# Layer 0 of a four-layer kernel: the first convolution one step later, and the small projection's copy at the head of ScalarE's step 0

## The chip, the core and the metric

The kernel runs on one core of a Trainium2 chip. The core has five engines that each work through their own list of instructions in order and wait for one another by semaphores: TensorE (PE, matrix products), VectorE (DVE), ScalarE (ACT, activation functions and copies), GpSimd (POOL) and SyncE (SP, which issues the DMAs here). The metric is the time of one execution on the device in microseconds (us), as a median over several runs.

## The reference

Four layers follow each other on an image of 2 x 128 channels x 64 x 64. The change lies in the first, layer 0: a Mamba block that is run over the 4096 pixels in four orders (by rows and by columns, each forward and reversed) for each of the two images.

```python
xz = x @ W_in.T;  xh, z = jnp.split(xz, 2, axis=-1)      # 256 + 256 channels
xc = depthwise_conv(xh, conv_w, taps=4) + conv_b
xh = silu(xc)
x_dbl = xh @ W_xp.T                                      # the small projection
dt = softplus(x_dbl[..., :8] @ W_dt.T + b_dt)
Bm, Cm = x_dbl[..., 8:24], x_dbl[..., 24:40]
dA = exp(dt[..., None] * A)                              # 256 channels x 16 states
dBu = dt[..., None] * Bm[:, :, None, :] * xh[..., None]
h_t = dA_t * h_{t-1} + dBu_t                             # a scan over 4096 pixels
y = einsum(h, Cm) + xh * Dp
y = y * silu(z)                                          # the gate
out = y @ W_out.T                                        # then fused over the four orders
```

Before it stands a layernorm over the channels. Layers 1 to 3 (two attention layers and another Mamba layer) are not touched.

## The kernel before

**Tiling.** A chunk is 512 consecutive pixels of one order of one image; there are 2 images x 4 orders x 8 chunks = 64 chunks, numbered 0 to 63. Of each eight, the orders alternate: chunks 0 to 7, 16 to 23, 32 to 39 and 48 to 55 run forward, the others reversed. The 256 channels x 16 states of a chunk are cut into 16 units of 128 partitions x 1024 elements, one unit for each step of the loop (`for s in range(16)`). The order of instructions on each engine is the order of the program text: the loop stands in a manual schedule, and nothing reorders it.

**One step `s` of chunk `c`** issues, in this order: on GpSimd the input term of unit s+2 (`s_dbu`, L330); on VectorE the scan of unit s (`s_scan`, L374), then what the table `V` holds for the step, then the product of unit s-1 with C (`s_hc`, L386; for units 0, 5, 9, 11 and 14 it is on GpSimd instead, L384); on ScalarE the decays of unit s+1 (`s_da`: two exponentials, L343), a correction of one column that carries the state from the chunk before (`s_fix`, L355 and L358), a copy of the last state (`s_hst`, L379), and then what the table `A` holds for the step; on TensorE the sums over states (`s_y`, L397, four units in two halves) and what the table `M` holds for the step, and in odd steps the spreading of C for the two next units (`s_pc`, L363).

**Where units wait for each other.** The decays have two buffers (PSUM), so the decays of unit s+1 wait for the end of scan s-1. The input terms have three, so that of unit s+3 waits for scan s. The sums of units 0 to 7 go to one PSUM bank `y`, which VectorE reads in step 10 (the gate of the first half, `yg_(0)`, L404), and those of 8 to 15 to the same bank, which VectorE reads in step 1 of the next chunk (`yg_(1)`, L404). The pairs of units are summed in steps 3, 5, 8, 9, 12, 14, 15 and, for the last pair, in step 1 of the next chunk: a pair waits for both products.

**Preparing later chunks.** The tables hold the work for the next chunk (`new`) and the one after it (`nxt`). All of it passes through one PSUM bank, `misc`: a matmul writes it, and another engine has to read it before the next matmul may write. For `nxt`: the convolution with its projection of channels 0 to 127 (`px(0)`, four matmuls that the trace shows as eight, L228) in step 8, its copy by ScalarE (`x_(0)`, L237) in step 9; `px(1)` in step 10 and `x_(1)` in step 12; the silu of both in step 13 (`xsilu`, L251); the small projection (`pd`, L267) at the end of step 15. For `new`: in step 0, behind decays, correction and state copy, ScalarE's copy of the small projection (`xd_`, L272), with two DMA stores to DRAM by SP (`rows`); then TensorE's `pt(0)` (L287) that reads this copy, in step 0, `pt(1)` in step 1, the absolute values (`abs_`, L294), `exp` and `ln` in steps 1 to 3, `pt` again in 4 and 5, `dt_` on VectorE (L306) in 5 and 6. TensorE's `pt(0)` stands ahead of the sums of the last pair in step 1. Forward chunks also gate `z` in step 8 (`zsilu`, L255, with two loads of an activation table).

**Layernorm chunks.** In chunks 0 to 3 and 15 to 22 part of the layernorm for later pixels runs as well (`ln`: `center` in step 12, `sub` on VectorE in 13, `square` in 14, `var` and `keep` in 14 and 15), and in the chunk after each of them (1 to 4 and 16 to 23) the rest (`lp`: `ln` and `exp` in step 3, `rows` in 6, `scale` in 7, `mul` on VectorE in 8, `affine` on ScalarE in 10).

## Time and profile before

| | us |
|---|---|
| median of 5 runs (6806.72 to 6814.91) | 6812.0 |
| the profiled execution | 6806.72 |
| its span on the core | 6804.9 |
| layer 0 within the span, first scan to last (57.2 to 3470.6) | 3413.4 |
| VectorE idle from 57 to 3468 | 142.5 |
| GpSimd idle from 57 to 3468 | 142.2 |

The page of the profile has a table of busy times, the span in slices, the chain of waits, and groups of instructions by line. A group's row reads: line, engine, operation, out<-in by the program's names, shapes, count | busy us, mean ns of one | idle time of the engine just before it, and what ended that idle time. A timeline row reads: start us, duration us, engine, line, operation, out<-in, shapes, count, and in brackets the engine's idle time before it with what ended it. The granted clock (PEclk) is the share of TensorE's full clock that the core let through.

### The profile page before, as it was taken

To read this page: it belongs to the slowest core of one execution; us is meant where nothing else is said; L and a number is where in the kernel's file an instruction comes from. 1 tells how busy PE (TensorE), PEld (TensorE's weight loads), DVE (VectorE), ACT (ScalarE), POOL (GpSimd) and SP (SyncE) were. 2 spreads that over 40 slices of the span, in tenths; PEclk is the share of its full clock that TensorE was granted. 3 is DMA by queue.
4 is the path that set the end of the run, shared out by engine and by line. 5 is a ranking of instruction groups with operands and counts; after the bars stand their busy time and mean duration, and the time that the engine had idled before them with its cause. 6 is when DMAs were issued, how large, how long until landed. Compare 5 with 4: busy or idle time off the path is not lost. (4 is left out here: it accounts for less than half of the span.)

```text
span 6804.9 us, 67303 instructions
## 1 busy us (share of the span) xinstructions
PE 5996.8 (88%) x20652; PEld 2820.5 (41%) x20652; DVE 5523.6 (81%) x4499; ACT 4457.0 (65%) x7666; POOL 5359.8 (79%) x2487
## 2 busy tenths in 40 slices
PE   8888888888888888888879999999999997888888
PEld 2222222222222222222238887787788884222222
DVE  7999999999999999999966665565566675787777
ACT  7887788877788777887745664555456554434342
POOL 6899998899999999999956664555566666777776
PEclk7777777777777777777779999999999998988888
DMA  6555655566566656565630000000000001222222
GB/s 170 138 149 145 158 147 137 139 156 147 145 157 152 154 144 156 151 154 145 150 91 2 4 4 1 1 1 1 1 1 13 1 1 61 74 72 71 90 75 67
DMA packets 352652, 616.51 MB, mean 91 GB/s; under 512 B 72473, under 2 KB 74786, under 8 KB 351650
## 3 DMA queue, kind: packets, MB, share of 16 engines
q1 hardware_dynamic: 351552, 610.44, 35.0%
q8 instruction: 162, 2.65, 0.2%
q14 instruction: 200, 1.64, 0.1%
q10 hardware_dynamic: 738, 1.78, 0.1%
HBM read 496.45 MB, written 115.47 MB: 90 GB/s over the span
## 5 line engine op out<-in xcount | busy, mean ns | idle before, releaser
L330 POOL TENSOR_TENSOR dbu<-dus,bs 128x1024 f32<-128x1024 f32 x1024 | 2401.5, 2370 | 154.6 <-DVE h L374 138.4
L374 DVE TENSOR_TENSOR_SCAN h<-da,hst,dbu 128x1024 f32<-128x1024 f32 x896 | 2092.7, 2343 | 76.1 <-ACT dbu L358 72.7
L343 ACT ACTIVATE da<-dts,aneg 128x512 f32<-128x512 f32 (+1 forms) x2048 | 1411.4, 689 | 443.7 <-DVE h L374 404.7
L890 POOL TENSOR_TENSOR sum<-sum,sc 128x1024 f32<-128x1024 f32 x384 | 906.1, 2360 | 497.6 <-ACT sc L885 494.0
L852 ACT COPY sc<-s 128x512 f32<-128x512 f32 x1024 | 597.0, 584 | 868.8 <-PE s L847 754.3
L859 DVE TENSOR_TENSOR mx<-mx,s 128x512 f32<-128x512 f32 x896 | 610.0, 681 | 569.4 <-ACT sc L852 568.4
L847 PE MATMUL s<-q,k 128*128 128x256 f32 x4096 | 1058.0, 382 | 11.7 <-ACT q L833 8.4
L902 PE MATMUL av<-sc,v 128*128 128x256 f32 x4096 | 1049.7, 379 | 2.3 <-ACT sc L885 2.3
L397 PE MATMUL y<-hc,cst 128*32 128x512 f32 x4096 | 813.3, 763 | 177.5 <-DVE hc L386 104.1
L386 DVE TENSOR_TENSOR hc<-h,pc 128x1024 f32<-128x1024 f32 x704 | 843.1, 1198 | 0.1
L847 PEld LDWEIGHTS s<-q,k 128*128 128x128 f32 x4096 | 781.2, 192 | 146.2 <-issue 36.6
L902 PEld LDWEIGHTS av<-sc,v 128*128 128x128 f32 x4096 | 769.1, 190 | 103.2 <-ACT sc L885 3.7
L384 POOL TENSOR_TENSOR hc<-h,cs 128x1024 f32<-128x1024 f32 x320 | 756.9, 2365 | 1.3 <-issue 1.3
L363 PE MATMUL pc<-xd,sel 16*128 16x512 f32 x1024 | 713.0, 788 | 4.4 <-DVE hc L386 3.9
L1217 POOL TENSOR_TENSOR A<-A,D 128x1024 f32<-128x1024 f32 x224 | 525.7, 2364 | 225.5 <-DVE D L1222 201.6
L882 DVE TENSOR_TENSOR sc<-sc,pm 128x1024 f32<-128x1024 f32 x512 | 620.9, 1213 | 0.9 <-PE pm L878 0.9
L885 ACT ACTIVATE sc<-sc 128x1024 f32<-128x1024 f32 x512 | 542.1, 1059 | 8.6 <-DVE sc L882 8.1
L287 PE MATMUL misc<-xd,w_dt 9*128 9x512 f32 x504 | 389.8, 862 | 161.0 <-ACT x L426 85.1
L1210 ACT ACTIVATE A<-dtr,aneg 128x1024 f32<-128x1024 f32 (+1 forms) x256 | 245.8, 1031 | 380.6 <-PE y L1242 363.1
L397 PEld LDWEIGHTS y<-hc,cst 128*32 128x32 f32 x4096 | 105.1, 117 | 743.5 <-issue 332.0
L1228 DVE TENSOR_TENSOR A<-A,q 128x1024 f32<-128x1024 f32 (+1 forms) x256 | 276.8, 1081 | 148.7 <-PE q L1194 148.6
L1194 PE MATMUL q<-xs,lb 32*128 32x512 f32 x896 | 331.6, 713 | 72.0 <-DVE D L1204 65.7
(263 smaller groups left out, 8056.9 us busy)
## 6 DMA issues: line engine op xcount, KB each, us to landing
dts<-ddt SPq DMA_DIRECT2D x512, 256.0 KB, 5.4
dus<-ddu SPq DMA_DIRECT2D x512, 256.0 KB, 5.0
bs<-rows SPq DMA_DIRECT2D x1024, 64.0 KB, 4.9
cs<-rows SPq DMA_DIRECT2D x1024, 64.0 KB, 3.2
ddt<-dt SPq DMA_DIRECT2D x128, 256.0 KB, 2.0
ddu<-dtu SPq DMA_DIRECT2D x128, 256.0 KB, 4.1
dtr<-ddt SPq DMA_DIRECT2D x448, 64.0 KB, 1.9
rx<-ddx SPq DMA_DIRECT2D x448, 64.0 KB, 1.9
```

The source lines that it names most:

```text
L330: nc.gpsimd.tensor_mul(t, self.dus[q], _bc(self.bs[g], 1, [P, 2, T]))
L343: act(t[:, i, sl], self.dts[q][:, i, sl], AF.Exp, scale=an[:, g, 2 * q + i : 2 * q + i + 1])
L363: mm(t, lhsT=sel[32:48, 4 * g : 4 * g + 4, :].rearrange("p n d -> p (n d)"), rhs=self.xd[32:48, :], start=True, stop=True)
L374: nc.vector.tensor_tensor_scan(ho, ai, bi, init, ALU.mult, ALU.add)
L384: nc.gpsimd.tensor_mul(t, self.h[u], _bc(self.cs[gq(u)[0]], 1, [P, 2, T]))
L386: nc.vector.tensor_mul(t, self.h[u], _bc(self.pc[u // 2], 1, [P, 2, T]))
L397: mm(self.y[q // 2][r : r + 32, :], lhsT=sum4, rhs=self.hc[u][:, i, :], start=False, stop=(u % 8 >= 6), skip_group_check=True)
L847: mm(p[:, o, :], lhsT=j.k[m // 8][:, m % 8 * P : m % 8 * P + P], rhs=self.q, start=True, stop=True)
L859: nc.vector.tensor_max(self.mx, self.s[0][:, 0:2, :] if u == 1 else self.mx, self.p[u])
L882: nc.vector.tensor_sub(s, s, _bc(self.pm[:, :], 1, [P, 4, NQ]))
L890: nc.gpsimd.tensor_add(self.sum, self.s[0] if w == 1 else self.sum, self.s[w])
L902: mm(self.av, lhsT=self.job.v[m // 8][:, m % 8, :], rhs=self.s[u // 2][:, m % 4, :], start=(m == 0), stop=(m == 31))
```

## The change

Three edits in the loop over chunks. `px(0)` of `nxt` moves from table entry 8 to 9 and its copy `x_(0)` from 9 to 10, behind `affine` where there is one. `xd_` leaves the table and is called at the head of ScalarE's part of step 0, ahead of the decays of unit 1. The block with `y0` and `s_y` is written ahead of ScalarE's part instead of behind it.

```diff
                 if new is not None:
-                    A[0] = (new.xd_,)
                     M[0], A[1] = lambda: new.pt(0), (lambda: new.abs_(0),)
...
                 if nxt is not None:
-                    M[8], A[9] = lambda: nxt.px(0), (lambda: nxt.x_(0),)
+                    M[9], A[10] = lambda: nxt.px(0), (lambda: nxt.x_(0),)
                     M[10], A[12] = lambda: nxt.px(1), (lambda: nxt.x_(1),)
...
-                    A[10] = (lp.affine,)
+                    A[10] = (lp.affine, *A.get(10, ()))
...
                     if s in G:
                         G[s]()
 
+                    if s in (3, 11):
+                        c.y0(s // 11)
+                    for cy, e in ((c, s), (old, s + 16)):
+                        for u in pairs.get(e, ()) if cy is not None else ():
+                            cy.s_y(u)
+                            cy.s_y(u + 1)
+
+                    if s == 0 and new is not None:
+                        new.xd_()
                     if c1 is not None:
                         c1.s_da(u1)
                         c1.s_fix(u1)
...
                     for f in A.get(s, ()):
                         f()
 
-                    if s in (3, 11):
-                        c.y0(s // 11)
-                    for cy, e in ((c, s), (old, s + 16)):
-                        for u in pairs.get(e, ()) if cy is not None else ():
-                            cy.s_y(u)
-                            cy.s_y(u + 1)
                     if s in M:
                         M[s]()
```

In the built program TensorE's list changes in one place of each chunk (the eight matmuls of `px(0)` stand behind the sums of units 6 and 7 instead of ahead of them), ScalarE's in two (`xd_` ahead of the decays in step 0, `x_(0)` one step later). The lists of VectorE, GpSimd and SP keep their order, and no instruction is added or removed.

## The prediction

> **What bounds the kernel now.** The edits touch layer 0 alone, so I first took its stretch of the span in the table of windows (columns: PE, PEld, VectorE, ScalarE, GpSimd busy, granted clock, DMA share, GB/s), then the waits of VectorE and GpSimd in it.

> ```profile
> 57.00:3468.00 3411.00, 2887.47 (x7750) 797.15 (x7750) 3268.47 (x2003) 2746.68 (x5231) 3268.77 (x1470) 0.77 0.60 148
> ...
> POOL dbu L330 <- DVE h L374: 138.4, 135, 2.5
> ...
> DVE h L374 <- ACT dbu L358: 72.7, 128, 1.4
> DVE dt L404 <- PE y L397: 38.5, 34, 2.3
> DVE dt L404 <- issue: 18.2, 9, 2.5
> ```

> VectorE and GpSimd are each busy for 3268 of 3411 us (96%) and idle for 142; GpSimd's idle time is nearly all a wait for the scan, so VectorE leads. Its idle time is what an edit can win: 72.7 us before scans, for ScalarE's correction (L358), and 57.1 before the gate (L404), for the sums. Nothing above that can be gained; but any new wait of VectorE adds to the time at once.

> Next I read where these waits lie, chunk by chunk, in the timeline. The gate waits 34.2 us in step 1 and 22.9 in step 10; in step 10 nearly all of it (22.7) is in the eleven chunks 1 to 4 and 16 to 22. The scan waits 22.4 us in step 5 (24 chunks, mostly reversed) and 29.1 in step 15.

> Step 0 of chunk 21, which stands for the twelve chunks 1 to 4 and 16 to 23:

> ```profile
> 1198.79 2.89 PE L267 MATMUL misc<-xs,m 128*73 128x512 f32 x4
> ...
> 1197.07 0.26 ACT L175 ACTIVATE r<-misc,eps 128x4 f32<-128x4 f32 x1
> 1197.22 1.40 ACT L343 ACTIVATE da<-dts,aneg 128x512 f32<-128x512 f32 x2
> 1198.56 0.28 ACT L355 ACTIVATE df<-aneg,dts 128x4 f32<-128x4 f32 x1
> 1198.94 0.39 ACT L358 ACTIVATE dbu<-hst,dbu,df 128x1 f32<-128x1 f32 x1
> ...
> 1201.72 0.68 ACT L272 ACTIVATE xd<-misc,vec 73x512 f32<-73x512 f32 x1 [2.31 <-PE misc L267]
> ...
> 1200.49 2.34 DVE L374 TENSOR_TENSOR_SCAN h<-da,hst,dbu 128x1024 f32<-128x1024 f32 x1
> 1204.64 0.69 DVE L404 TENSOR_TENSOR dt<-sz,y 128x512 f32<-128x512 f32 x1 [1.80 <-PE y L397]
> ```

> ScalarE uses the time in which the small projection (L267) is not ready for the decays of unit 1, and still waits 2.31 us for it afterwards. Scan 1 runs at 1200.49, well ahead of the copy.

> **The copy first in step 0.** One instruction of 0.68 us moves ahead of two decays, the correction and the state copy; it adds no work. Its two stores go out on SP at the same place of SP's list; what reads them is issued from step 8 on, 27 us later, so they cost nothing. What counts is what is now queued behind a wait for the small projection: the decays of unit 1, and scan 1 behind them.

> Chunk 21: ScalarE is free at 1197.33 and now waits for the projection until 1201.72. The copy ends at 1202.40, where it ends today, so `pt(0)`, the sums and the gate's input gain nothing. Decays to correction take 2.11 us (1197.22 to 1199.33): ready at 1204.5. Scan 1 starts 4.0 us late, ends at 1206.8, the gate follows without its 1.80 of wait, and scan 2 comes at about 1207.4 instead of 1205.24: 2.2 lost. I did this sum at each of the 62 chunk boundaries with ScalarE's free time, the projection's end, scan 1 and the gate's wait: 2.2 in eleven of these twelve and 1.5 in chunk 16, together 26.

> Reversed chunks are of two kinds. Chunk 59 (first three lines) and chunk 28 (last two; of the projection's four matmuls the stretch that I asked for holds the last alone):

> ```profile
> 3209.05 2.98 PE L267 MATMUL misc<-xs,m 128*73 128x512 f32 x4
> 3212.27 0.68 ACT L272 ACTIVATE xd<-misc,vec 73x512 f32<-73x512 f32 x1
> 3213.40 2.34 DVE L374 TENSOR_TENSOR_SCAN h<-da,hst,dbu 128x1024 f32<-128x1024 f32 x1
> ...
> 1576.95 0.59 PE L267 MATMUL misc<-xs,m 128*73 128x512 f32 x1
> 1579.69 0.68 ACT L272 ACTIVATE xd<-misc,vec 73x512 f32<-73x512 f32 x1
> ```

> In chunk 59 the projection ends at 3212.03 (2.0 us after scan 0 begins), at a granted clock of 0.57; in 28 it ends at 1577.54 (0.1 after), at 1.00. Late: the copy ends at 3212.75, 0.2 earlier than today, the correction at 3214.9, scan 1 is 1.5 late, and ScalarE is through with step 0 2.0 later. Step 5 of such chunks waits for ScalarE (1.06 here), so ScalarE's lag passes to VectorE. 19 of the 27 reversed boundaries are late, lags of 1.5 to 2.2, 38 in all, less 0.6 of gate waits: +37. Early: nothing is lost, and in six chunks a gate wait of 1.26 goes, of which 0.56 comes back in step 5 (the wait there of chunk 28, which has no gate wait): 6 x 0.7 = -4. Together +33.

> Forward chunks without layernorm: 17 boundaries, 8 late by 0.5 to 0.9 net (+6.0), 9 early with gate waits of 0.5 to 1.06 that go (-7.4): -1.4. The six chunks that begin a row of eight: +2.5. The copy's move sums to 26 + 33 - 1.4 + 2.5 = +60. Bounds: if every projection is late, 26 + 27 x 2.1 + 17 x 0.9 + 4 = +102; if every one is early, see the first rival.

> **The convolution behind the sums.** Eight matmuls of L228 move behind the sums of units 6 and 7, and one copy of 0.69 us goes from step 9 to 10. Chunk 20:

> ```profile
> 1171.06 1.94 PE L397 MATMUL y<-hc,cst 128*32 128x512 f32 x8
> 1172.92 5.63 PE L228 MATMUL misc<-xnt,wk 128*128 128x512 f32 x8
> 1178.49 1.06 PE L397 MATMUL y<-hc,cst 128*32 128x512 f32 x8
> 1180.53 3.70 PE L228 MATMUL misc<-xnt,wk 128*128 128x512 f32 x8
> ...
> 1178.59 0.69 ACT L237 ACTIVATE xs<-misc,vec 128x512 f32<-128x512 f32 x1 [4.02 <-PE misc L228]
> ...
> 1179.68 0.69 DVE L404 TENSOR_TENSOR dt<-sz,y 128x512 f32<-128x512 f32 x1 [2.46 <-issue]
> ```

> In the eleven chunks, gate and decays of unit 11 both wait behind the first convolution: 2.46 us, and 0.56 more at scan 11. With the sums ahead, the gate's input is there at 1174.9. But TensorE does the same work without a gap from 1171 to the mean for the layernorm in step 12, which ends at 1188.2, and VectorE's subtraction of step 13 needs it; that subtraction starts at 1188.8 today. So of 3 us only 0.6 to 0.8 can be kept: 11 x 0.7 = -8. The bounds are -3.0 and +1.0 a chunk (the convolution at half clock for two rows more).

> In the 20 forward chunks the step-10 and step-11 waits are 0.2 to 0.4 us; I take -0.2 each, -4. Queued behind the copy in step 10 are now the decays of unit 12. In reversed chunks there is no wait to win, and the convolution starts later: chunk 59 runs it at 3237.99, and the product of unit 7 ends at 3242.06, so it starts at 3243.1 after a gap in TensorE. At full clock (3.70) after a slow start it ends at about 3247.7, its copy at 3248.4, and the deadlines hold: the spread of C for unit 10 is due at 3250.4, the second convolution's copy at 3252.3. Cover: 0. At half clock throughout it takes 3.70 x 1.94/1.06 = 6.8, ends at 3249.9, and with 1.1 for the spread and 3.70 for the second convolution the second copy ends 2.4 later than today; scan 15 waits 0.63 for ScalarE already, so at most 2.4 is lost. Range 0 to 2.4 x 31 = 74; I take 0, since the clock was 0.55 up to 1178.5 and 1.00 right after it in chunk 20, that is, it rose within such a convolution.

> [...]

> Moving the block of `s_y` in the text changes no engine's order by itself: 0.

> **Sum.** 60 - 8 - 4 = +48 on the profiled execution's 6806.7 (span 6804.9 and 1.8 around it): 6855. The median stands 5.3 above it: 6860.

> **Rivals.** First (not slower, it can be faster): the later convolution fills TensorE's list through steps 11 to 13, the clock stays up and every projection is early. Then reversed chunks give -5, forward ones -8, the twelve lose 1.45 less each (half of 2.89), +9, the convolution -12: -16, 6796. It decides once the projection runs at clock 1.00 at nearly all boundaries. For it: chunk 28; against: the two kinds alternate today, and a longer chunk shifts them. Chance 0.14. Second (no change): the clock stays up in plain chunks, but the twelve keep their 26: 26 - 5 - 8 - 12 = +1, 6813. Chance 0.14. Third (slower still): the convolution runs at half clock in the reversed chunks: +48 + 74 = 6934 at most. For it: the gap; against: the rise in chunk 20. Chance 0.17. The change not doing what it says is part of my forecast: at the boundaries where the copy waits for the projection today, putting it first makes it no earlier.

> **Chances.** My forecast, late copies at half the boundaries, has 0.55 and its own range 6830 to 6890. With the rivals the range is 6796 to 6918: it leaves out the lower half of the first and the upper half of the third, some 0.15. Differences under 0.2% (13.6 us) can't be told from none: faster 0.12 (the first rival but for its end near zero), same 0.16 (that end and the second), slower 0.72 (forecast and third).

> **What would show it.** ScalarE's copy (L272) waiting for L267 in most chunks, 1.5 to 4.4 us each, against 26.7 us in all today; the first decays of step 0 behind it; scan 1 waiting for L358 by 3 to 4 us in the twelve chunks; the gate's waits gone; the subtraction (L161) waiting for its mean. I am wrong if L272 waits for less than 60 us in all, or if L386 and scan 15 in reversed chunks wait much longer than today.

## The result and the profile after

| | before | after |
|---|---|---|
| median, us | 6814.76 (47 runs) | 6815.38 (27 runs) |
| ratio, 95% interval | | 1.0003 [0.9998, 1.0009] |
| profiled execution, us | 6806.72 | 6798.98 |
| layer 0, first scan of chunk 0 to first scan of chunk 63 | 3363.5 | 3375.1 |

No change that can be measured, where I had forecast 48 us more. Layer 0 itself did get longer, by 11.6 us in the profiled executions. Both figures repeat within 0.8 us in a second profile of each kernel (3363.7 and 3374.3), so this is no accident of one execution.

The table of windows for layer 0 after the change (columns as before: PE, PEld, VectorE, ScalarE, GpSimd busy, granted clock, DMA share, GB/s), and the list of waits:

```profile
57.00:3468.00 3411.00, 2885.17 (x7727) 790.11 (x7727) 3256.15 (x1998) 2730.09 (x5222) 3258.79 (x1465) 0.78 0.60 148
```

```profile
ACT xs L237 <- PE misc L228: 118.0, 53, 3.7
DVE h L374 <- ACT dbu L358: 69.5, 117, 1.3
ACT xs L237 <- PE y L390: 67.7, 56, 2.0
ACT xd L272 <- PE misc L267: 56.3, 19, 5.0
DVE h L374 <- ACT hst L379: 42.8, 12, 4.5
...
DVE xc L161 <- PE misc L157: 16.6, 12, 2.0
...
DVE hc L386 <- PE y L397: 8.6, 18, 0.8
```

(A row of waits: who waited and for whom, us in total, number of waits, longest us.) Three things are to be seen. VectorE's busy time in the same stretch fell by 12.3 us: so much more of it is now waiting. The waits of the gate (L404) are gone from the list, 57 us of them. In their place stand twelve waits of a scan for ScalarE's state copy (42.8 us), the subtraction (L161, 16.6) and the products (L386, 8.6). And the small projection's copy (L272) waits only 19 times, not "in most chunks".

Sorted by kind of chunk, each from its first scan to the next chunk's (plain means without layernorm; "first" are the six chunks after chunk 0 that begin a row of eight and have none; a projection is late if it ends over 0.5 us after scan 0 begins):

| | twelve layernorm chunks | 17 forward plain | 6 first | 27 reversed | late at 50 plain boundaries |
|---|---|---|---|---|---|
| before, us | 681.7 | 900.1 | 301.5 | 1429.2 | 31 |
| after, us | 694.9 | 897.0 | 306.8 | 1425.0 | 1 |
| difference | +13.2 | -3.1 | +5.3 | -4.2 | |
| predicted | +26 - 8 | -1.4 - 4 | +2.5 | +33 | |

The error of 37 us lies in the reversed chunks. The step into chunk 60 in the timeline of the kernel after; scan 15 and scan 0 stand as one row of two, so scan 0 begins at about 3273.6:

```profile
3271.20 1.94 PE L267 MATMUL misc<-xs,m 128*73 128x512 f32 x4
...
3271.35 4.59 DVE L374 TENSOR_TENSOR_SCAN h<-da,hst,dbu 128x1024 f32<-128x1024 f32 x2 [1.20 <-ACT dbu L358]
...
3273.40 0.68 ACT L272 ACTIVATE xd<-misc,vec 73x512 f32<-73x512 f32 x1
...
3276.97 2.35 DVE L374 TENSOR_TENSOR_SCAN h<-da,hst,dbu 128x1024 f32<-128x1024 f32 x1
...
3279.23 0.66 DVE L404 TENSOR_TENSOR dt<-sz,y 128x512 f32<-128x512 f32 x1
```

The projection takes 1.94 us, at a granted clock of 1.00, and ends before scan 0 begins. ScalarE copies it without a wait, scan 1 and the gate have none either. What is paid is the 1.20 in front of scan 15, where before it was 0.63 (ahead of chunk 59). The step into chunk 60 had its projection early before the change, too; the one into chunk 59, which the prediction shows as late, is now early:

```profile
3219.14 1.94 PE L267 MATMUL misc<-xs,m 128*73 128x512 f32 x4
```

It ends 0.6 us before scan 0 begins at 3221.63. Before, it took 2.98 us and ended 2.0 us after scan 0 began.

In a layernorm chunk (21, which begins at 1210.03) it went as I had worked it out:

```profile
1210.30 3.62 PE L267 MATMUL misc<-xs,m 128*73 128x512 f32 x4 [0.20 <-ACT r L175]
...
1213.96 0.68 ACT L272 ACTIVATE xd<-misc,vec 73x512 f32<-73x512 f32 x1 [3.71 <-PE misc L267]
1214.54 1.40 ACT L343 ACTIVATE da<-dts,aneg 128x512 f32<-128x512 f32 x2
...
1216.74 2.35 DVE L374 TENSOR_TENSOR_SCAN h<-da,hst,dbu 128x1024 f32<-128x1024 f32 x1 [3.25 <-ACT hst L379]
...
1219.01 0.66 DVE L404 TENSOR_TENSOR dt<-sz,y 128x512 f32<-128x512 f32 x1
```

The copy waits 3.71 us for the projection, the decays of unit 1 stand behind it, and scan 1 waits 3.25; the gate no longer waits.

### The profile page after: what moved, and what is told of

It is laid out like the page before. It is cut to its first block, busy times and chain, and to the rows that moved or that the text cites. A ratio compares the mean times of both kernels' runs of the same rounds, so it can differ in the third digit from the quotient of the medians.

```text
span 6797.2 us, 67302 instructions
## 1 busy us (share of the span) xinstructions
PE 5991.3 (88%) x20652; PEld 2812.8 (41%) x20652; DVE 5516.3 (81%) x4499; ACT 4445.8 (65%) x7666; POOL 5360.7 (79%) x2487
## 5 line engine op out<-in xcount | busy, mean ns | idle before, releaser
L330 POOL TENSOR_TENSOR dbu<-dus,bs 128x1024 f32<-128x1024 f32 x1024 | 2401.1, 2370 | 165.6 <-DVE h L374 148.4
L374 DVE TENSOR_TENSOR_SCAN h<-da,hst,dbu 128x1024 f32<-128x1024 f32 x896 | 2093.0, 2343 | 114.9 <-ACT dbu L358 69.5
L343 ACT ACTIVATE da<-dts,aneg 128x512 f32<-128x512 f32 (+1 forms) x2048 | 1410.3, 689 | 369.6 <-DVE h L374 331.2
L397 PE MATMUL y<-hc,cst 128*32 128x512 f32 x4096 | 908.1, 761 | 209.5 <-DVE hc L386 202.5
L386 DVE TENSOR_TENSOR hc<-h,pc 128x1024 f32<-128x1024 f32 x704 | 844.0, 1199 | 11.8 <-PE y L397 8.6
L363 PE MATMUL pc<-xd,sel 16*128 16x512 f32 x1024 | 696.9, 771 | 1.6 <-DVE hc L386 1.3
L397 PEld LDWEIGHTS y<-hc,cst 128*32 128x32 f32 x4096 | 126.7, 120 | 881.9 <-DVE hc L386 462.1
L287 PE MATMUL misc<-xd,w_dt 9*128 9x512 f32 x504 | 349.7, 779 | 131.7 <-ACT x L426 59.6
```

What stands on the lines that cost most here:

```text
L330: nc.gpsimd.tensor_mul(t, self.dus[q], _bc(self.bs[g], 1, [P, 2, T]))
L343: act(t[:, i, sl], self.dts[q][:, i, sl], AF.Exp, scale=an[:, g, 2 * q + i : 2 * q + i + 1])
L363: mm(t, lhsT=sel[32:48, 4 * g : 4 * g + 4, :].rearrange("p n d -> p (n d)"), rhs=self.xd[32:48, :], start=True, stop=True)
L374: nc.vector.tensor_tensor_scan(ho, ai, bi, init, ALU.mult, ALU.add)
L386: nc.vector.tensor_mul(t, self.h[u], _bc(self.pc[u // 2], 1, [P, 2, T]))
L397: mm(self.y[q // 2][r : r + 32, :], lhsT=sum4, rhs=self.hc[u][:, i, :], start=False, stop=(u % 8 >= 6), skip_group_check=True)
```

## The experiments

The theory at this point: the copy in front costs time where the projection is late, the later convolution makes the projections of the plain chunks early, and in the layernorm chunks it gains more than I gave it. The rival: the copy's move itself, with the delays that it makes, changed the clock. The first four kernels take the change apart.

**The convolution's move alone.**

```diff
-                    M[8], A[9] = lambda: nxt.px(0), (lambda: nxt.x_(0),)
+                    M[9], A[10] = lambda: nxt.px(0), (lambda: nxt.x_(0),)
...
-                    A[10] = (lp.affine,)
+                    A[10] = (lp.affine, *A.get(10, ()))
```

> The kernel before with the convolution's move alone (px(0) in step 9, x_(0) in step 10); the small projection's copy stays behind the decays. Theory (the convolution's move keeps TensorE at full clock until the small projection, and the copy's move costs about 2 us in each of the twelve layernorm chunks): at nearly all of the 50 plain boundaries the small projection ends within 0.5 us of scan 0, as with the whole change (1 late of 50), against 31 late of 50 before; layer 0 is 10 to 25 us shorter than with the whole change and 0 to 15 us shorter than before, so 6795 to 6812 us beside 6814. Rival (the early projection comes from the copy's move, the convolution's move does nothing outside the layernorm chunks): 20 or more of the 50 boundaries stay late and the time is that of before within 5 us.

Measured: 6826.95 against 6807.87, 1.0027 [1.0015, 1.0038]. One projection of 50 is late, so this move makes them early, and the rival falls. But the time did not follow: the twelve get shorter by 25.8 us, the reversed chunks longer by 29.4 and the first ones by 9.6. A reversed chunk in its timeline, steps 9 to 15 of chunk 60 (which begins at 3275.87):

```profile
3309.19 5.40 PE L228 MATMUL misc<-xnt,wk 128*128 128x512 f32 x8
...
3315.57 3.70 PE L228 MATMUL misc<-xnt,wk 128*128 128x512 f32 x8
...
3320.17 0.69 ACT L237 ACTIVATE xs<-misc,vec 128x512 f32<-128x512 f32 x1 [1.45 <-PE y L390]
...
3322.21 1.22 DVE L386 TENSOR_TENSOR hc<-h,pc 128x1024 f32<-128x1024 f32 x1 [0.59 <-PE y L397]
...
3327.84 1.94 PE L267 MATMUL misc<-xs,m 128*73 128x512 f32 x4
...
3328.07 4.59 DVE L374 TENSOR_TENSOR_SCAN h<-da,hst,dbu 128x1024 f32<-128x1024 f32 x2 [1.27 <-ACT dbu L358]
```

The first convolution takes 5.40 us, the second starts late, its copy holds ScalarE for 1.45 (the row names L390, the matmuls that follow the second convolution on TensorE), a product waits 0.59 and scan 15 waits 1.27. And in step 0 of the same chunk the small projection's copy still stands behind the decays:

```profile
3273.38 1.94 PE L267 MATMUL misc<-xs,m 128*73 128x512 f32 x4
...
3275.99 1.41 ACT L343 ACTIVATE da<-dts,aneg 128x511 f32<-128x511 f32 x2 [0.24 <-DVE h L374]
...
3278.10 0.68 ACT L272 ACTIVATE xd<-misc,vec 73x512 f32<-73x512 f32 x1
...
3278.82 2.07 PE L287 MATMUL misc<-xd,w_dt 9*128 9x512 f32 x2 [2.46 <-ACT xd L272]
...
3280.83 1.94 PE L397 MATMUL y<-hc,cst 128*32 128x512 f32 x8
...
3282.83 0.69 DVE L404 TENSOR_TENSOR dt<-sz,y 128x512 f32<-128x512 f32 x1 [1.26 <-PE y L397]
```

The projection is ready at 3275.3 and is copied at 3278.1; `pt(0)` and the sums follow it, and the gate waits 1.26. Early projections alone help nobody as long as the copy comes last in step 0.

**The copy's move alone.**

```diff
-                    A[0] = (new.xd_,)
...
+                    if s == 0 and new is not None:
+                        new.xd_()
                     if c1 is not None:
                         c1.s_da(u1)
```

> The kernel before with the copy's move alone. Theory: the small projection stays late at about half of the 50 plain boundaries, ScalarE waits for it with the decays queued behind, and the +60 us of the prediction's arithmetic appear: 6850 to 6880 us, with about 26 of them in the twelve layernorm chunks and 33 in the reversed ones. Rival (the lost time at ScalarE is made up elsewhere and the sum of the prediction was wrong by itself): 6815 to 6830 us, layernorm chunks longer by less than 15 us in all.

Measured: 6839.56, 1.0050 [1.0038, 1.0063]. Now all 27 reversed projections are late. Its list of waits:

```profile
ACT xd L272 <- PE misc L267: 132.3, 54, 5.2
DVE h L374 <- ACT hst L379: 87.0, 45, 4.5
```

This is the picture that I had predicted for the change as a whole: a wait of the copy at nearly every boundary and 87 us of scans behind it. Yet it costs 31.5 us in layer 0 and not 60 to 102. The idle time of VectorE by kind of chunk and step shows why (us; sums over the chunks of the kind, worked out from the gaps in the traces):

| | before | convolution alone | copy alone | after |
|---|---|---|---|---|
| reversed, step 1: scan | 0 | 0 | 46.2 | 0 |
| reversed, step 1: gate | 8.1 | 31.5 | 0 | 0 |
| reversed, step 5: scan | 19.9 | 0 | 2.2 | 6.5 |
| reversed, step 13: product | 0 | 10.2 | 0 | 6.0 |
| reversed, step 15: scan | 15.7 | 30.4 | 15.7 | 30.3 |
| reversed, all steps | 52.0 | 76.5 | 64.5 | 47.3 |
| layernorm, step 1: scan | 0 | 0 | 39.6 | 46.2 |
| layernorm, step 1: gate | 17.3 | 14.0 | 0 | 0 |
| layernorm, steps 10 and 11: gate and scan | 28.9 | 0 | 23.2 | 0 |
| layernorm, step 13: subtraction | 0 | 10.6 | 0 | 15.2 |
| layernorm, all steps | 55.7 | 31.2 | 72.7 | 69.4 |

In reversed chunks a late scan 1 takes the place of waits in steps 1, 3 and 5: 46 us new, 33 gone. And the two moves repair each other: the convolution makes the projection early, so the copy in front has no wait (46.2 to 0); the copy in front takes the gate's wait away that the convolution alone brings (31.5 to 0). The singles sum to 15.4 + 31.5 = 46.9 us in layer 0; together they cost 11.6.

**The whole change, but with the copy in its old place in the twelve layernorm chunks.** Against the kernel after:

```diff
+                    if lp is not None:
+                        A[0] = (new.xd_,)
...
-                    if s == 0 and new is not None:
+                    if s == 0 and new is not None and lp is None:
                         new.xd_()
```

> The whole change, but in the twelve chunks that finish a layernorm (1 to 4, 16 to 23) the copy keeps its old place behind the decays. Theory: the twelve chunks lose the wait of scan 1 (47 us over 12 chunks, of which 26 us were a net loss) and the rest stays as with the change: 15 to 30 us under the change, 6785 to 6800 us. Rival (the layernorm chunks are bound by TensorE through step 13 anyway, the 47 us only replace other waits): within 8 us of the change.

Measured: 6769.07, 0.9949 [0.9936, 0.9962]: faster than the kernel before. Layer 0 is 3337.1 us (3375.1 with the whole change), the twelve 655.6. Against the kernel after this is 39.3 us less in the twelve alone, and so that is the price of the copy in front there once the convolution stands late: 46.2 of scans and 4.4 more before the subtraction, less 11.8 of gate waits (this kernel's own, in the twelve).

**The copy alone, with `px(1)` issued twice in plain chunks**, to keep TensorE busy late in the chunk without the convolution's move.

```diff
+                    if ln is None and lp is None:
+                        M[10] = lambda: (nxt.px(1), nxt.px(1, nxt.px_))
```

> The copy's move alone, and in chunks without layernorm work the second convolution (four matmuls, 3.7 us at full clock) is issued twice over the same bank, which adds work for TensorE and nothing for any other engine. Theory (what makes the projection early is a TensorE that is busy through steps 10 to 13 and so keeps its clock): late projections at plain boundaries fall under 15 of 50 and the time falls under that of the copy's move alone by 15 us or more, in spite of the added matmuls. Rival (order and not the clock makes the projection early): late boundaries stay at 25 or more and the time is that of the copy's move alone or up to 30 us longer.

Measured: 6855.81, 1.0072 [1.0060, 1.0084]. The late projections fell from 37 to 17 of 50, between the two expectations, so more work does bring them forward; but the time is 16 us above that of the copy alone, as the rival allowed, since the extra work holds back the sums that the products wait for:

```profile
DVE hc L386 <- PE y L397: 32.2, 19, 2.2
```

The added work is too large to separate the two effects; the experiment with the z projections below adds less.

**The later convolution in the twelve layernorm chunks alone**, nothing else changed.

```diff
-                    M[8], A[9] = lambda: nxt.px(0), (lambda: nxt.x_(0),)
+                    w = 9 if lp is not None else 8
+                    M[w], A[w + 1] = lambda: nxt.px(0), (lambda: nxt.x_(0),)
...
-                    A[10] = (lp.affine,)
+                    A[10] = (lp.affine, *A.get(10, ()))
```

> The kernel before with the convolution's move in the twelve chunks that finish a layernorm alone (1 to 4, 16 to 23), the copy in its old place everywhere. Theory (the convolution's move wins 26 us in the layernorm chunks and loses 29 us in the reversed ones, where it had no wait to remove): layernorm chunks 682 to 656 us, the reversed ones as before (1429 within 5), late projections in the reversed chunks as before (about 19 of 27), layer 0 shorter by 20 to 30 us; 6780 to 6795 us beside 6808. Rival (the gain in the layernorm chunks hangs on what the move does to the clock in the whole layer): layernorm chunks gain less than 13 us.

Measured: 6775.56, 0.9953 [0.9941, 0.9966]. The twelve take 656.4 (-25.3), the reversed 1429.6 (+0.4), and the projections are late as before (28 of 50). So the gain in the twelve is their own, and no matter of the clock elsewhere. The timeline and the windows of its chunk 20, which begins at 1125.49:

```profile
1156.53 3.34 PE L397 MATMUL y<-hc,cst 128*32 128x512 f32 x16
1159.80 3.70 PE L228 MATMUL misc<-xnt,wk 128*128 128x512 f32 x8
```

```profile
1146.00:1159.40 13.40, 10.83 (x26) 2.40 (x26) 13.40 (x10) 11.57 (x23) 13.33 (x7) 0.50 0.50 132
1159.40:1179.00 19.60, 16.82 (x56) 5.93 (x52) 18.57 (x12) 16.85 (x34) 18.90 (x9) 1.00 0.85 218
```

The clock rises at 1159.4, 33.9 us into the chunk (38.0 with the whole change, where the chunk begins with the copy's wait). Before, the convolution took 5.63 us, at a granted clock of 0.65 over its length, as the clock rose only 37.7 us into the chunk. Here it finds the clock up and takes 3.70. That is the 1.9 us a chunk which my sum "TensorE does the same work" left out.

**The split version, with `x_(1)` copied in step 13 instead of 12 where the next chunk is reversed.** It is aimed at the wait that remains, of scan 15.

```diff
                     A[13] = (nxt.xsilu,)
+                    if new.rev and ln is None:
+                        A[13] = (*A.pop(12), nxt.xsilu)
```

> The split version (whole change, copy in its old place in the layernorm chunks), and in reversed chunks without layernorm the second convolution's copy moves from step 12 to step 13, behind the decays of unit 14. Theory (with the convolution later, ScalarE waits in step 12 for the second convolution with the decays of unit 14 queued behind, which makes the wait of scan 15 in reversed chunks 1.27 us instead of 0.63): the wait of scan 15 falls from 49 us to about 30 us in all and the reversed chunks by 10 to 17 us; 5 to 20 us under the split version. Rival (the wait of scan 15 is set by the table loads and silu of step 13 and not by the copy ahead of them): the wait stays at 45 us or more, the time within 5 us of the split version.

Measured: 6772.73, 0.9950 [0.9935, 0.9964]. VectorE's wait in step 15 falls from 49.1 to 35.6 us over layer 0, but the reversed chunks lose only 4.8. Part of what they gain in step 15 (30.1 to 20.4) comes back before scan 5 (5.6 to 10.5). Layer 0 is 10.5 us shorter than in the split version, and the time is the same within the intervals: the wait moved as the theory said, the time as the rival did. The wait of that copy more than halves, from 67.6 us in the split version to

```profile
ACT xs L237 <- PE y L390: 28.6, 27, 2.0
```

**The copy alone, with two z projections (results not read) in step 13 where the next chunk is reversed.** Against the kernel with the copy alone:

```diff
+                    if new.rev and ln is None:
+                        M[13] = lambda: (nxt.pz(0), nxt.pz(1, nxt.pz_))
```

> The copy's move alone, and in the chunks ahead of a reversed chunk two matmuls of the z projection are issued in step 13 into the free bank and never read: work for TensorE where it was idle, on nobody's path. Theory (the projection is early when TensorE was busy through step 13 and so ran at full clock): late projections in reversed chunks fall from 27 of 27 to under 8, the granted clock in the last 5 us of these chunks is over 0.9, and the reversed chunks take 1400 to 1430 us against 1441 with the copy's move alone. Rival (the order of the convolution makes it early, the clock follows): 20 or more stay late and the reversed chunks take 1441 us or longer.

Measured: 6816.33, 1.0014 [1.0005, 1.0023], 10.5 us above the kernel before as timed beside it, where the copy alone was 31.7 above, although TensorE does more. Of the 27 reversed projections 16 are late, where with the copy alone all 27 were; the result lies between the two expectations for the count, and the reversed chunks (1426.0) are where the theory had them. The waits behind the copy:

```profile
ACT xd L272 <- PE misc L267: 99.9, 54, 5.2
DVE h L374 <- ACT hst L379: 55.0, 31, 4.5
```

(132.3 and 87.0 with the copy alone.) The granted clock over the last 5 us ahead of the reversed chunks is 0.89 on the mean, 0.50 with the copy alone (0.64 before, 1.00 after). So two z projections more in step 13 raised the clock ahead of the projection from 0.50 to 0.89, but not at every boundary: 16 of 27 stay late.

**The kernel before and the kernel after once more**, without an edit, to see what repeats.

> The kernel before, profiled once more. Theory: layer 0 repeats within 3 us (3363.5 us from the first scan of chunk 0 to that of chunk 63), and the rest of the span varies by 10 us or more, which is why 12 us in layer 0 did not show in the ratio. Rival: layer 0 itself varies by 10 us or more between executions, so the 12 us are no effect of the change.

> The whole change once more, profiled and timed. Theory: layer 0 repeats (3375.1 us from the first scan of chunk 0 to that of chunk 63, within 3 us) and is 12 us longer than before, while the time after layer 0 differs between executions by up to 27 us (3317 to 3342 us in the traces so far), so that the ratio lies between 0.999 and 1.003. Rival: the time after layer 0 is shorter with the change by about as much as layer 0 is longer, in every execution: it stays near 3317 us in this trace too.

Measured: the kernel before 6797.09 in its one run, the kernel after 6815.7 against 6811.52, 1.0004 [0.9995, 1.0013]. Layer 0 repeats within 0.2 and 0.8 us, and the sums of every kind of chunk within 2.2. What is left of the span from the end of the last scan does not repeat: 3334.3 and 3324.0 us before, 3316.7 and 3332.9 after.

**The later copy of `x_(1)` in all chunks without layernorm.** Only the condition of the experiment above changes.

```diff
-                    if new.rev and ln is None:
+                    if ln is None:
```

> As the version that copies the second convolution in step 13 in the reversed chunks, but in all chunks without layernorm. Theory (the wait of scan 15 in the forward chunks, 0.63 us, also comes from the copy ahead of the decays): forward chunks fall from 895 us by 5 to 12 us, the time by as much. Rival (in forward chunks the second z projection of step 13 needs the bank, and its matmuls and copy become late instead): forward chunks stay or grow.

Measured: 6786.89, 0.9961 [0.9947, 0.9975]. The forward plain chunks grew from 894.7 to 910.8 us, and 15 projections are late, against 5 in the version above, seven of the 15 at full clock. The z projection (L241) now waits 29.2 us for that copy, 19 times, and never in the split version. The rival is right, and the later copy shortens reversed chunks alone.

## Why the prediction was wrong

The time lies in the range, but the forecast was a slower kernel, 6830 to 6890, and nothing of the sort came. It is the second rival in kind: the clock stays up in the plain chunks and the twelve keep their loss. That its 6813 lies 2 us from the median is luck: it had +1 us for what is +11.6 in layer 0. Step by step:

- **"Late copies at half the boundaries"** is the step that failed. It took the clock at which each projection ran before and kept it for the changed kernel. In the twelve traces, 398 projections at plain boundaries were early, all at full clock (1.94 us), and 202 late, 190 of them below it. The convolution's move alone turned 31 late ones into 1. The clock in the 5 us around the projection ahead of chunk 59, before and after:

```profile
3207.00:3212.00 5.00, 4.80 (x9) 1.04 (x9) 4.37 (x3) 4.51 (x12) 5.00 (x3) 0.58 1.07 223
```

```profile
3217.00:3222.00 5.00, 3.84 (x10) 0.93 (x10) 3.73 (x3) 4.83 (x11) 5.00 (x3) 1.00 1.07 229
```

  0.58 against 1.00, although TensorE is busy for longer in the first window; what differs lies ahead of it. The first two rivals had this in them, at a chance of 0.14 each, and the first named the way: the later convolution fills TensorE's list and the clock stays up. With it, the +33 of the reversed chunks became -4.2. Where the clock was up, and with which work, stands below the list.
- **"6 x 0.7 = -4" for early projections in reversed chunks**: the right mechanism for all 27 of them, but not against the kernel before. The gate's wait that goes is mostly one that the later convolution would have brought (31.5 us alone).
- **The twelve chunks, +26 for the copy.** The mechanism is right in every part: copy waits for the projection, decays behind it, scan 1 late (predicted 4.0, measured 46.2 / 12 = 3.9 us), gate without a wait. The price was mis-sized, +39.3 measured with the convolution late: the scan's wait is as predicted, but the gate wait that it replaces is 11.8 us and not the 1.80 a chunk of chunk 21 (21.6; all twelve had 17.3 before), and 4.4 come back before the subtraction. With the convolution in its old place, the case that my sum was made for, the price is +17.6: 39.6 of scans, less 17.3 of gate waits and 5.7 of waits in steps 10 and 11.
- **The convolution in the twelve, "only 0.6 to 0.8 can be kept"**: -26 measured, not -8, at 2.1 to 2.2 us a chunk inside the bound of -3.0 that I gave. The subtraction does wait for its mean, as predicted (10.6 us in the twelve with the convolution alone), but TensorE gets there earlier, as its clock rises earlier (33.9 us into chunk 20 against 37.7, above).
- **"Cover: 0", "I take 0" for the convolution in reversed chunks**: alone it costs +29.4, of which 24.5 can be seen as idle time of VectorE; it took 5.40 us in chunk 60, between the 3.70 and the 6.8 that I had worked out. My 0 rested on the rise of the clock in chunk 20, where TensorE ran without a gap from 1171.00 on (busy for 17.20 us of 17.20); the slow start after a gap, some 0.9 us on the 3.70, was my estimate. In the change 14.6 us in step 15 and 6.0 in step 13 stand against 8.1 of gate waits and 21 of waits in steps 3 and 5 gone. The bound of 74 also counted 31 such chunks, where 27 boundaries were counted for the copy.
- **Forward and first chunks**: -3.1 and +5.3 against -5.4 and +2.5. Small, and the first ones have the same wait in step 15 (1.3 to 4.7).

Of the signs that I named, two of the kind "I am wrong if" came true: the copy waited 56.3 us, under 60, and L386 and scan 15 in reversed chunks waited longer (0 to 6.0 and 15.7 to 30.3).

The clock records of the traces show how the convolution's move reaches the projection. They hold two values alone, 0.50 and 1.00, in stretches of whole multiples of 3.41 us (3850 stretches of layer 0 in twelve traces). TensorE in chunk 58, the one ahead of chunk 59; three rows before (busy at half clock, the long full stretch, what follows it), then the long full stretch after:

```profile
3177.10:3187.30 10.20, 10.20 (x26) 2.78 (x27) 10.20 (x8) 6.22 (x17) 9.95 (x5) 0.50 0.23 82
3187.30:3204.37 17.07, 14.24 (x50) 4.13 (x48) 17.07 (x12) 12.26 (x25) 17.07 (x9) 1.00 0.89 210
3204.37:3211.20 6.83, 4.89 (x11) 1.01 (x8) 6.20 (x4) 6.37 (x13) 6.83 (x4) 0.50 0.77 171
```

```profile
3203.70:3224.18 20.48, 18.67 (x57) 5.24 (x56) 18.62 (x12) 16.38 (x34) 20.48 (x10) 1.00 0.81 185
```

Before, it ends at 3204.37, ahead of the projection at 3209.05; after, it starts later in the chunk and lasts past the projection at 3219.14. So it is in all 27 chunks ahead of a reversed one: before, it starts 29.6 us into the chunk (median) and ends 2.1 to 11.1 us before the chunk does, and the clock is up again for the projection in the 8 early ones alone; after, it starts at 33.9 and ends 1.7 to 8.5 us into the next chunk. The last 3.41 us of the stretch before, in which TensorE is busy for 1.30, and the leanest 3.41 us of the stretch ahead of the projection after, with 2.43:

```profile
3200.96:3204.37 3.41, 1.30 (x8) 0.29 (x8) 3.41 (x3) 3.36 (x7) 3.41 (x2) 1.00 0.44 139
```

```profile
3213.94:3217.35 3.41, 2.43 (x14) 0.39 (x12) 3.41 (x3) 3.38 (x4) 3.41 (x2) 1.00 0.42 127
```

With the convolution late, the sums behind it come later too and fill what was a gap in TensorE's work (2.76 us, up to 3203.07). Busy time alone does not separate the cases: in the row from 3177.10 TensorE is busy without a gap for 10.2 us at half clock, and in the kernel before 113 of the 282 windows of 3.41 us after which the clock stayed at half were busy from end to end. TensorE's busy time in each 3.41 us without the spread of C (L363, 16 rows) and the product `pt` (L287, 9 rows) separates them better, here summed over layer 0 in all twelve traces. At half clock this rest was over 2.8 us in 1882 of the 1926 windows after which the clock rose, and in 23 of the 3175 after which it did not. At full clock it was under 1.4 us in 1807 of the 1924 windows after which it fell, and in 40 of the 4912 after which it did not. From step 11 on, the leanest window of the 27 chunks held 0.7 to 1.4 us of such work before and 1.5 to 2.0 after. These sums are read from traces, and no kernel was built to test the two bounds: they say how the windows of these traces divide, not why the clock moved.

One thing stays open. Layer 0 is 11.6 us longer in the first pair of profiles and 10.6 in the second, but the ratio of 1.0003 is +2 us, with an upper end of 9 in the wider of the two intervals (0.0013 x 6812). Something after layer 0 may be given back; with a rest of the span that moves by 10 to 16 us from one execution of the same kernel to the next, these runs can't show it. In the other edited kernels, too, the medians differ from layer 0's own change by up to 12 us (the split version: -26.4 in layer 0, -38.8 in the medians).

## What to carry to other kernels

A matmul's duration in the profile holds for the clock at which it ran (the four of the projection ahead of chunk 59 took 2.98 us at 0.64 before and 1.94 at 1.00 after), and here moving TensorE's work in one step changed that clock a third of a chunk later (the convolution at 3200.73, the projection at 3219.14, in a chunk of 53.7 us): before costing a wait for a matmul, find in the clock's row where its full stretch starts and ends, and price both cases. Two moves that each make a kernel slower can repair each other (46.9 us apart, 11.6 together), so time them alone and together, and sort the result by kind of chunk, because one edit can win in one kind and lose in another. Here the kinds wanted different orders: the convolution later in layernorm chunks alone (0.9953), or everywhere with the copy in front in plain chunks only (0.9949), beats the kernel before; the change as a whole does not.
